# Cross-attention on one core: scores by seven block products in a reordered round

## The chip, the cores and the metric

The kernel runs on one core of a Trainium2 chip. A core has five engines, each with its own instruction list that it works through in order: PE (TensorE: matrix products, and PEld, its weight loads), DVE (VectorE), ACT (ScalarE), POOL (GpSimd) and SP (SyncE, which here issues the DMA transfers). They meet only through semaphores. The metric is the device time of one execution in microseconds (us).

## What is computed

For each of 64 batches, with x of 256 x 512, c of 256 x 384 and a hidden width H of 512, in fp32:

```python
text_p = x @ W_text + b_text
audio_p = c @ W_audio + b_audio
Q = layer_norm(text_p, g1, beta1)
K = layer_norm(audio_p, g2, beta2)
alpha = softmax(Q @ K.T / sqrt(512))
y = (alpha @ audio_p) @ W_out + b_out + x
out = layer_norm(y, g_out, beta_out)
```

## The kernel before

**Stages.** The loop `for b in range(B - 2)` is a software pipeline: round b works on five batches at once. It projects batch b+2 to its keys (`k2`) and queries (`q2`), scores batch b (`at`), forms the context of batch b-1 (`last`) and the output of batch b-2 (`old`), and normalises the output rows of batch b-3 (`settled`). Rounds 3 to 60 are alike; 0 to 2 fill the pipeline, round 61 and the code behind the loop drain it.

**Products.** The key projection and the output projection (class `Thirds`; the output's instance is `old.o`) use a scheme with 15 block products 171 columns wide instead of 18. Their parts are called `one` (into N0, N1), `two` (M0, M1), `three` (T), `four` (T, M, L) and `five` (N, M, U); N, M, L and the bank of T and U are four banks of PSUM that key and output projection share, one after the other. Steps between them (`after_one`, `after_three`, `after_four`, `after_five`) copy or combine those banks on VectorE and ScalarE; `seed` fills M with the bias. The query projection (class `Fork`) uses seven products of two chunks, 256 columns wide, in two banks: `one`, `seven`, `six`, `five`, `rest`. The sums of blocks that these schemes need on the activation side are formed on GpSimd: `Sides` (csum for the keys, zsum for the output, seven steps, L340) and `SumX` (xsum, four steps, L311). The scores (`score`, L712) are plain: 2 row tiles x 4 chunks, 256 columns wide. The context is `context_one` and `context_two` (L778). Each fp32 product appears as two instructions in the trace.

**Transposes.** The rows of q, k and e go to DRAM (`store`) and come back in squares (`fetch`, four transfers); VectorE then turns them with 32 x 32 block transposes (`turn`, `turn_e`). `affine` applies gain and shift to the turned q and k on ScalarE, chunk by chunk.

**Norms.** `rstd_of` (L400 to L404) forms the inverse root on GpSimd: a small sum, then a power of -0.5. The rows of q and k are scaled by it on ScalarE (`normalise`). An output row gets `totals` (GpSimd), `deviations` (ScalarE), `shift` (VectorE, L962), `scale_row` (ScalarE, L976) and `lift_rows` (GpSimd, L980).

**Softmax.** `maxima` (VectorE, L722), `exponentials` (ScalarE with accumulated sums, L729), `reciprocals` (VectorE, L739), `divide_e` (ScalarE, L743).

**Order.** Every engine's list is in the order of the statements, written by hand; nothing reorders it. Pools of PSUM and SBUF tiles have one to four buffers each, and the next use of a buffer waits for the readers of the last one.

Of the kernel before, what the change touches and what calls it, by code (L numbers as in the profile page):

```python
# [9 lines left out]
F32 = mybir.dt.float32  # L10
# [12 lines left out]
def kernel(  # L23
# [78 lines left out]

    ident = const.tile([P, P], F32, tag="ident", name="ident")
    make_identity(nc, ident)
    nhalf = const.tile([P, 2], F32, tag="nhalf", name="nhalf")
# [158 lines left out]
    def means(rows, n, name):  # L264

        m = const.tile([P, n], F32, tag=name, name=name)
        for k in range(n):
            junk = work.tile([P, H], F32, tag="junk", name="junk")
# [137 lines left out]

    class Projection:
# [25 lines left out]
        def square(self):  # L433

            self.var = small.tile([P, self.nt], F32, tag=f"var{self.name}", name="var")
            for t in range(self.nt):
                junk = work.tile([P, H], F32, tag="junk", name="junk")
# [8 lines left out]
        def scales(self):  # L446
            if self.centred:
                self.r = rstd_of(self.var, self.nt)
                return
# [12 lines left out]
        def normalise(self):  # L462
            for t in range(self.nt):
# [39 lines left out]
        def affine(self, gam, bet, chunks=range(HC)):  # L503
            for k in chunks:
# [6 lines left out]
                )  # L511

# [3 lines left out]
    class Thirds(Projection):  # L516
# [47 lines left out]

        def after_one(self):
            n1 = self.room("n1")
            nc.vector.tensor_copy(n1, self.N1)
            dve(self.T, self.N0, n1, ALU.subtract)

        def after_three(self):  # L570
            t = self.room("t")
            nc.vector.tensor_copy(t, self.T)
            dve(self.L0, self.M0, t, ALU.add)
            dve(self.L1, self.M1, t, ALU.subtract)

        def after_four(self):
            m = self.room("m")
            dve(m, self.M1, self.delta, ALU.subtract)
            dve(self.U, self.M0, m, ALU.subtract)

        def after_five(self):
            u, n = self.room("u"), self.room("n", 2)
            nc.scalar.copy(u, self.U)
            nc.scalar.copy(n, self.N)
            dve(middle(self.rows[:, 0]), self.T, u, ALU.add)
            dve(ends(self.rows[:, 1]), self.M, n, ALU.add)
            self.noted = u, n
# [3 lines left out]

        def last_middle(self):
            u, n = self.noted
            d = self.room("d")
            nc.gpsimd.tensor_tensor(d, n[:, 0], n[:, 1], ALU.subtract)
            nc.gpsimd.tensor_tensor(middle(self.rows[:, 1]), u, d, ALU.add)

        def leave_plus(self, x, between):
            rows = self.rows
            u, n, v = self.room("u"), self.room("n", 2), self.room("d")  # L600
            dve(n, self.M, ends(x[:, 1]), ALU.add)
            dve(u, self.U, middle(x[:, 1]), ALU.add)
            dve(v, self.N0, u, ALU.add)
            between()
            self.totals = small.tile([P, 2, 2], F32, tag="totals", name="totals")
            self.last_sum(1, 0, inner, v[:, :W1], self.N1[:, :W1], ALU.subtract)
            self.last_sum(1, 1, ends, self.N, n, ALU.add)
            u = self.room("u")
            dve(u, self.U, middle(x[:, 0]), ALU.add)
            self.last_sum(0, 0, inner, self.T[:, :W1], u[:, :W1], ALU.add)  # L610
            self.last_sum(0, 1, ends, self.L, ends(x[:, 0]), ALU.add)
# [12 lines left out]
    class Fork(Projection):  # L624
# [38 lines left out]

        def after_six(self):
            dve(self.q3, self.R, self.s7, ALU.add)
            dve(self.R, self.R, bt_step, ALU.add)
# [7 lines left out]
        def rest(self):  # L674
            self.product(3, self.R)
            self.product(2, self.q1)
            self.product(4, self.q3)

        def square(self):
            self.var = small.tile([P, 2], F32, tag="varq", name="var")  # L680
            for t in range(2):
                junk = work.tile([P, H], F32, tag="junk", name="junk")
# [8 lines left out]
        def normalise(self):  # L691
            for t in range(2):
                nc.scalar.mul(self.rows[:, t, :], fork[t], self.r[t])

    class Attention:
# [23 lines left out]

        def maxima(self):  # L720
# [3 lines left out]
        def exponentials(self):  # L724

            self.e = once.tile([P, LT, S], F32, tag="e", name=f"e_{self.b}")
            self.den = small.tile([P, LT], F32, tag="den", name="den")
            for t in range(LT):
# [12 lines left out]
        def divide_e(self):  # L741
            for t in range(LT):
# [26 lines left out]
        def context_one(self):  # L769
# [3 lines left out]
            for j in range(2):  # L773
                for s in range(ST):
                    self.context_product(self.ps_z1[:, j, :], j, s)

        def context_product(self, ps, j, s):
# [4 lines left out]
                start=(s == 0),  # L782
                stop=(s == ST - 1),
            )

        def context_two(self, s):
# [3 lines left out]
            self.context_product(self.ps_z2, 2, s)  # L790
# [14 lines left out]
        def start_products(self, tag="zsum", pool=once):  # L805

            sides = Sides(self.zT, tag, pool).add()
# [18 lines left out]
        def sums(self, lo=0, n=LT):  # L826
# [4 lines left out]
            for t in self.summed:  # L831
                junk = work.tile([P, D], F32, tag="junk", name="junk")
                nc.scalar.activation(
                    junk, self.y[:, t, :], AF.Identity, scale=-1.0 / D, accum_out=self.nm[:, t : t + 1]
                )

# [647 lines left out]
```

## Time and profile before

| | |
|---|---|
| median of 3 runs | 1369.07 us (1368.69 to 1369.11) |
| the profiled execution | 1368.85 us |
| its span, first to last instruction | 1367.1 us |
| DMA moved | 322.02 MB |
| DMA queue of SP, share of 16 engines | 79.9% |

In a row of the order of time stand the start and the length in us, the engine, the line, the operation, out<-in, shape, and how many instructions were merged; in square brackets the idle time before it and who ended it. A group row has the number of instructions, busy us, the mean of one in ns, and the idle time before them. A row of a window has the window, its length, then busy us and count of PE, PEld, DVE, ACT and POOL, the granted TensorE clock, the DMA share and GB/s. A DMA row has the size in KB and the us to landing. Matrix products are pipelined, so one instruction's length is longer than the distance from its start to the next one's; the distance is what counts.

### The profile page before, as it was taken

The page shows a single profiled execution, that of the slowest core. Times are in us where ns is not written, and L with a number is a line of the kernel's source. Part 1 is how long each engine was busy: PE and PEld are TensorE (multiplying, and loading weights), DVE is VectorE, ACT ScalarE, POOL GpSimd, SP SyncE. Part 2 cuts the span into 40 slices and gives each one's busy share as a digit, 9 for nine tenths or more (in the row PEclk, how much of TensorE's full clock was granted, in tenths as well). Part 3 has the DMA queues.
Part 4 walks back from the last instruction along what each step waited for, and adds up shares of the span by engine and source line. Part 5 has one row for each costly group of instructions (what it writes and reads, how often), then busy time and mean ns, then how long its engine had stood idle before and what let it go on. Part 6 is the DMA issues. An engine that isn't in the chain of part 4 may idle for free. (4 is left out here: it accounts for less than half of the span.)

```text
span 1367.1 us, 26408 instructions
## 1 busy us (share of the span) xinstructions
PE 1355.5 (99%) x7429; PEld 1241.0 (91%) x7429; DVE 1113.6 (81%) x2689; ACT 1089.9 (80%) x2688; POOL 1158.6 (85%) x1927
## 2 busy tenths in 40 slices
PE   9999999999999999999999999999999999999997
PEld 5889999999999999999999999999999999999995
DVE  6778888888888888888888888888888888888868
ACT  5778888888788788888888887887888888888884
POOL 5788888888888888888888888888888888888865
PEclk9999999999999999999999999999999999999999
DMA  8788878877888878788789778888887888887773
GB/s 229 215 238 252 246 233 242 242 244 233 246 242 236 244 240 249 227 250 242 240 241 248 236 236 247 234 239 245 243 245 235 242 248 237 240 238 233 220 221 107
DMA packets 449096, 322.02 MB, mean 236 GB/s; under 512 B 153781, under 2 KB 381621, under 8 KB 448950
## 3 DMA queue, kind: packets, MB, share of 16 engines
q1 hardware_dynamic: 448854, 320.20, 79.9%
q8 instruction: 60, 0.98, 0.3%
q14 instruction: 86, 0.70, 0.2%
q10 hardware_dynamic: 96, 0.13, 0.0%
HBM read 203.57 MB, written 116.65 MB: 234 GB/s over the span
## 5 line engine op out<-in xcount | busy, mean ns | idle before, releaser
L712 PE MATMUL ps_sc<-kT,qT 128*128 128x256 f32 x1024 | 260.9, 379 | 0.0
L340 POOL TENSOR_TENSOR zsum<-zsum,zT 128x256 f32<-128x256 f32 x305 | 193.4, 651 | 14.4
L712 PEld LDWEIGHTS ps_sc<-kT,qT 128*128 128x128 f32 x1024 | 186.3, 190 | 17.3 <-ACT zT L793 0.2
L778 PE MATMUL ps_z<-eT,c 128*128 128x256 f32 x768 | 186.3, 379 | 1.1 <-DVE eT L76 1.1
L644 PE MATMUL ps_f<-wtsum,xsum 128*128 128x256 f32 x756 | 183.9, 379 | 0.0
L340 POOL TENSOR_TENSOR csum<-csum,cT 128x256 f32<-128x256 f32 x310 | 172.9, 566 | 9.9
L778 PEld LDWEIGHTS ps_z<-eT,c 128*128 128x128 f32 x768 | 143.0, 190 | 18.0 <-DVE eT L76 1.5
L980 POOL TENSOR_TENSOR yr<-yr,beo 128x512 f32<-128x512 f32 x122 | 153.6, 1281 | 3.1 <-ACT yr L976 3.1
L644 PEld LDWEIGHTS ps_f<-wtsum,xsum 128*128 128x128 f32 x756 | 138.1, 190 | 14.1 <-issue 0.5
L404 POOL TENSOR_TENSOR rstd<-ve,nhalf 128x2 f32<-128x2 f32 x192 | 136.3, 710 | 16.0
L340 POOL TENSOR_TENSOR zsum<-zT 128x256 f32<-128x256 f32 x122 | 72.2, 592 | 85.3 <-ACT zT L796 85.3
L505 ACT ACTIVATE qT<-qT,columns 128x256 f32<-128x256 f32 x256 | 139.2, 594 | 2.5 <-DVE qT L76 2.5
L505 ACT ACTIVATE kT<-kT,columns 128x256 f32<-128x256 f32 x256 | 139.3, 595 | 2.0 <-DVE kT L76 1.1
L644 PE MATMUL ps_f<-wt,xT 128*128 128x256 f32 x504 | 129.4, 379 | 0.0
L729 ACT ACTIVATE e<-ps_sc,nmx 128x256 f32<-128x256 f32 x128 | 59.5, 469 | 62.8 <-DVE nmx L722 62.8
L962 DVE SCALAR_TENSOR_TENSOR yr<-yr,nm,go 128x512 f32<-128x512 f32 x124 | 104.1, 840 | 2.0 <-ACT junk L843 2.0
L644 PEld LDWEIGHTS ps_f<-wt,xT 128*128 128x128 f32 x504 | 92.9, 190 | 10.7 <-ACT ps_f L636 0.6
L514 DVE TENSOR_TENSOR ps_l<-ps_m,t 128x171 f32<-128x171 f32 x248 | 85.5, 345 | 16.9
L796 ACT COPY zT<-ps_z 128x256 f32<-128x256 f32 x64 | 23.8, 372 | 86.2 <-PE ps_z L778 86.2
L514 DVE TENSOR_TENSOR ps_f<-ps_f,s 128x256 f32<-128x256 f32 x126 | 54.5, 432 | 44.3 <-PE ps_f L644 40.9
L976 ACT ACTIVATE yr<-yr,rstd 128x512 f32<-128x512 f32 x122 | 87.4, 717 | 2.6 <-POOL rstd L404 1.1
L311 POOL TENSOR_TENSOR xsum<-xT 128x256 f32<-128x256 f32 x124 | 88.2, 733 | 0.0
(247 smaller groups left out, 3775.7 us busy)
## 6 DMA issues: line engine op xcount, KB each, us to landing
kd<-kr SPq DMA_DIRECT2D x64, 512.0 KB, 3.1
kq<-kd SPq DMA_DIRECT2D x256, 128.0 KB, 3.2
qd<-qr SPq DMA_DIRECT2D x64, 512.0 KB, 3.0
qq<-qd SPq DMA_DIRECT2D x256, 128.0 KB, 2.7
xq<-in_x_dram SPq DMA_DIRECT2D x252, 128.0 KB, 3.3
x<-in_x_dram SPq DMA_DIRECT2D x63, 512.0 KB, 4.7
out_dram<-yr SPq DMA_DIRECT2D x62, 512.0 KB, 4.0
cq<-in_ctx_dram SPq DMA_DIRECT2D x252, 96.0 KB, 3.3
```

The costliest lines, as they stand in the source:

```text
L311: self.engine.tensor_tensor(*step)
L340: nc.gpsimd.tensor_tensor(*step)
L404: nc.gpsimd.tensor_tensor(r, ve, nhalf[:, :n], ALU.pow)
L505: nc.scalar.activation(self.T[:, k, :], self.T[:, k, :], AF.Identity, bias=bet[:, k : k + 1], scale=gam[:, k : k + 1],)
L514: nc.vector.tensor_tensor(o, i0, i1, op)
L644: nc.tensor.matmul(place, lhsT=side, rhs=w, start=False, stop=True, skip_group_check=True)
L712: nc.tensor.matmul(self.sc[:, t, :], lhsT=self.q.T[:, k, bass.ts(t, P)], rhs=self.k.T[:, k, :], start=(k == 0), stop=(k == HC - 1),)
L729: nc.scalar.activation(self.e[:, t, :], self.sc[:, t, :], AF.Exp, bias=self.nmx[:, t : t + 1], accum_out=self.den[:, t : t + 1],)
L778: nc.tensor.matmul(ps, lhsT=c_rows[self.b][:, s, bass.ts(j, P)], rhs=self.eT[:, s, :], start=(s == 0), stop=(s == ST - 1),)
L962: nc.vector.scalar_tensor_tensor(row, row, self.nm[:, t : t + 1], go_sb, ALU.add, ALU.mult)
L976: nc.scalar.mul(self.y[:, t, :], self.y[:, t, :], self.r[t])
L980: nc.gpsimd.tensor_tensor(self.y[:, t, :], self.y[:, t, :], beo_sb, ALU.add)
```

## The change

Rounds 3 to 60 (`fast`) get a body of their own, in which the parts of all stages are interleaved statement by statement. In it:

- the scores are seven block products of two chunks, 128 columns wide (`score_part`). Their sums of blocks are formed on GpSimd, four of the queries in round b (`query_step`) and three of the keys one round earlier (`key_step`); PSUM blocks are copied by ScalarE (`copy_p1`, `copy_p7`) and added by VectorE (`add_p7`);
- inverse roots come from ScalarE, as exp(-0.5 ln(var + eps)) (`rstd_beside`), one pair for q and k together and one for the output; this holds in the other rounds too;
- an output row is scaled and lifted by one VectorE instruction (`settle`, the form of `shift`) in place of `scale_row` and `lift_rows`;
- the copies of N1 and T, two for the keys and two for the output, move from VectorE to ScalarE;
- the affine of the keys moves into the round before; e's fetch moves to the head of the next round.

In the diff, `y` is `old.o`. Besides, junk comes from a pool with one buffer, and the context products set their start flag once per bank. The loads, stores and fetches are as many as before. The core of the diff:

```diff
+    nc.scalar.preload_act_table_set("natural_log_exp_and_others")
...
+    def rstd_beside(var, n, by=1.0):
+        log = small.tile([P, n], F32, tag=f"log{n}", name="log")
+        nc.scalar.activation(log, var, AF.Ln, bias=eps, scale=by)
+        r = small.tile([P, n], F32, tag=f"rstd{n}", name="rstd")
+        nc.scalar.activation(r, log, AF.Exp, scale=-0.5)
+        return [r[:, t : t + 1] for t in range(n)]
...
+    def scales_of(a, b, var):
+        r = rstd_beside(var, 4)
+        a.r, b.r = r[:2], r[2:]
...
+        def copy_n1(self):
+            self.n1 = self.room("n1")
+            nc.scalar.copy(self.n1, self.N1)
+        def start_t(self):
+            dve(self.T, self.N0, self.n1, ALU.subtract)
...
-            t = self.room("t")
-            nc.vector.tensor_copy(t, self.T)
+            self.t = self.room("t")
+            nc.scalar.copy(self.t, self.T)
...
+        def key_sums(self):
+            T = self.k.T
+            t = once.tile([P, 3, 2, P], F32, tag="ksum", name="ksum")
+            b11, b12, b21, b22 = [self.block("k", j, m) for j in range(2) for m in range(2)]
+            self.ksteps = [
+                (t[:, 0:2], T[:, :, P:].rearrange("p (j c) s -> p j c s", j=2),
+                 T[:, :2, :].rearrange("p c (m s) -> p m c s", m=2), ALU.subtract),
+                (t[:, 2], b22, t[:, 0], ALU.subtract),
+                (b12, b21, t[:, 2], ALU.subtract),
+            ]
...
+        def query_sums(self):
+            s = once.tile([P, 3, 2, P], F32, tag="qsum", name="qsum")
+            a11, a21, a12, a22 = [self.block("q", j, m) for j in range(2) for m in range(2)]
+            self.steps = [
+                (s[:, 1], a11, a21, ALU.subtract),
+                (s[:, 0], a21, a22, ALU.add),
+                (s[:, 2], s[:, 0], a11, ALU.subtract),
+                (a21, a12, s[:, 2], ALU.subtract),
+            ]
...
+        def open_scores(self):
+            self.sc = p_at.tile([P, LT, S], F32, tag="at", name="ps_sc")
+            nc.vector.memset(self.sc[:, :, P:], 0.0)
+        def score_part(self, *parts):
+            for n in parts:
+                t, m = {7: (1, 1), 2: (0, 0), 4: (1, 0)}.get(n, (0, 1))
+                for c in range(2):
+                    nc.tensor.matmul(self.place(t, m), lhsT=self.qsides[n][:, c],
+                        rhs=self.ksides[n][:, c], start=False, stop=True, skip_group_check=True)
+        def copy_p1(self):
+            nc.scalar.copy(self.place(0, 0), self.place(0, 1))
+        def copy_p7(self):
+            self.s7 = once.tile([P, P], F32, tag="sc7", name="sc7")
+            nc.scalar.copy(self.s7, self.place(1, 1))
+        def add_p7(self, m):
+            dve(self.place(1, m), self.place(0, 1), self.s7, ALU.add)
...
+        if fast:
+            last.fetch_e()
+            k2.one()
+            old.context_two(0); old.context_two(1)
+            if b + 4 < B: load_c(b + 4)
+            k2.copy_n1()
+            k2.start_t()
+            old.copy_two()
+            settled.totals()
+            at.affine_queries(1)
+            cT[b + 3] = turn_c(b + 3)
+            at.affine_queries(0)
+            q2.six()
+            old.start_products(n=1)
+            k2.three()
+            k2.copy_t()
+            k2.two()
+            k2.start_l0()
+            at.affine_queries(2)
+            old.zsides.add(1)
+            q2.seven()
+            k2.start_l1()
+            at.query_sums()
+            at.query_step(0)
+            old.zsides.add(1)
+            at.affine_queries(3)
+            settled.deviation(0)
+            k2.four()
+            xT[b + 3] = turn_x(b + 3)
+            k2.take_m()
+            q2.after_seven()
+            settled.deviation(1)
+            at.query_step(1)
+            old.zsides.add(1)
+            k2.start_u()
+            k2.five()
+            k2.copy_n()
+            k2.copy_u()
+            at.open_scores()
+            q2.start_q3()
+            old.zsides.add(1)
+            at.query_step(2)
+            y.one()
+            y.copy_n1()
+            q2.step_r()
+            q2.five()
+            k2.leave_ends()
...
+            settled.last_deviation()
+            k[b + 1].turn([0])
+            k2.leave()
+            k[b + 1].turn([1])
+            y.start_t()
+            at.score_part(1, 7)
+            k2.square(var[:, 2:], [0])
+            at.copy_p1()
+            q2.after_five()
+            y.two()
+            at.copy_p7()
...
+            last.turn_e()
+            y.start_l0()
+            k2.middle_d()
+            settled.shift(1)
+            at.score_part(6)
+            at.add_p7(0)
+            q2.three()
+            settled.settle(1)
...
+            q2.square(var[:, :2], [0])
+            cs[b + 3].add(1)
+            at.score_part(3)
+            att[b + 1].affine_keys(3)
+            x_new.add(1)
+            scales_of(q2, k2, var)
+            at.score_part(2)
+            k2.normalise([0])
+            k2.normalise([1])
+            q2.normalise([0])
+            k2.seed()
...
+            at.maxima()
+            q2.normalise([1])
+            Fork.seed()
+            k2.store()
+            last.context_one()
+            settled.shift(0)
+            at.exponentials([0])
+            at.exponentials([1])
+            y.last_10()
+            at.reciprocals()
+            last.copy_one()
+            y.plus_middle(x_old, 0)
+            at.divide_e([0])
+            q2.store()
+            q3 = q[b + 3] = Fork(b + 3, x_new.of, wt_blocks)
+            q3.one()
+            x_new.add(1)
+            y.last_01(x_old)
+            k2.fetch()
...
+            y.last_00()
+            cs[b + 3].add(1)
+            Fork.clear()
+            q3.after_one()
+            at.store_e()
+            if b + 4 < B: att[b + 1].key_step(2)
+            q2.fetch()
+            settled.settle(0)
+            continue
```

More of the change, by code (lines that the diff above doesn't have):

```diff
@@ L431, in evict, with square @@
                 moments(self.mv, self.rows[:, t, :], t)
[L433 to L437, printed above, removed]
+        def square(self, var=None, tiles=range(2)):
+            if var is None:
+                var = small.tile([P, self.nt], F32, tag=f"var{self.name}", name="var")
+            self.var = var
+            for t in tiles:
+                junk = once.tile([P, H], F32, tag="junk", name="junk")
                 nc.scalar.activation(
@@ L672, in after_five, with three, two, four @@
             dve(self.q2, self.R, self.s7, ALU.add)
-        def rest(self):
[L675 to L682, printed above, removed]
+        def three(self):
+            self.product(3, self.R)
+        def two(self):
+            self.product(2, self.q1)
+        def four(self):
+            self.product(4, self.q3)
+        def rest(self):
+            self.three()
+            self.two()
+            self.four()
+        def square(self, var=None, tiles=range(2)):
+            if var is None:
+                var = small.tile([P, 2], F32, tag="varq", name="var")
+            self.var = var
+            for t in tiles:
+                junk = once.tile([P, H], F32, tag="junk", name="junk")
                 nc.scalar.activation(
@@ L722, in maxima, with exponentials @@
             nc.vector.tensor_reduce(self.nmx, self.sc, AX.X, ALU.max, negate=True)
[L724 to L728, printed above, removed]
+        def exponentials(self, tiles=range(LT)):
+            if 0 in tiles:
+                self.e = once.tile([P, LT, S], F32, tag="e", name=f"e_{self.b}")
+                self.den = small.tile([P, LT], F32, tag="den", name="den")
+            for t in tiles:
                 nc.scalar.activation(
```

334 lines of the change are left out of this document (255 added, 79 removed).

## The prediction

> **What bounds the kernel now.** I read the page first, then TensorE in order of time over one steady round, then all engines over ten rounds, then the start, where products 128 columns wide can be seen.
>
> ```profile
> span 1367.1 us, 26408 instructions
> ...
> PE 1355.5 (99%) x7429; PEld 1241.0 (91%) x7429; DVE 1113.6 (81%) x2689; ACT 1089.9 (80%) x2688; POOL 1158.6 (85%) x1927
> ```
>
> TensorE is busy for 99% of the span. A modelled duration can hide a wait, so I check the pace in the order of time:
>
> ```profile
> 303.92 0.74 PE L530 MATMUL ps_n<-wa,csum 128*128 128x171 f32 x4
> 304.50 0.74 PE L530 MATMUL ps_m<-wa,csum 128*128 128x171 f32 x4
> ...
> 306.23 1.89 PE L644 MATMUL ps_f<-wtsum,xsum 128*128 128x256 f32 x8
> 307.95 0.45 PE L530 MATMUL ps_u<-wa_thirds,csum 128*128 128x171 f32 x2
> ...
> 322.98 1.89 PE L778 MATMUL ps_z<-eT,c 128*128 128x256 f32 x8
> 324.70 0.74 PE L530 MATMUL ps_n<-wa,csum 128*128 128x171 f32 x4
> ```
>
> From start to start, four instructions of 171 columns take 0.58 us (0.145 each) and eight of 256 columns 1.72 us (0.215 each). A steady round has 56 wide ones (28 for q, 16 for scores, 12 for context) and 60 of 171 columns: 56 x 0.2155 + 60 x 0.1452 = 20.78 us, and the round lasts 324.70 - 303.92 = 20.78. TensorE issues without a gap. Whatever shortens its list pays in full, and a wait put into the list costs in full.
>
> ```profile
> 506.00:712.00 206.00, 206.00 (x1153) 191.72 (x1152) 170.78 (x417) 168.12 (x416) 179.38 (x298) 1.00 0.81 241
> ```
>
> 206 us are 9.91 rounds. So per round VectorE (third time) works 17.2 us, ScalarE 17.0 and GpSimd 18.1; each has over 2 us to spare. The granted clock is 1.00.
>
> **TensorE's part of the change.** Rounds b = 3 to 60, 58 of them, replace 16 instructions of 256 columns (8 products, two instructions each in the trace) by 7 blocks x 2 chunks x 2 = 28 of 128 columns. At full clock the trace has no such product of two ordinary operands. Nearest are the transposes of 128 columns at the start, and what follows them:
>
> ```profile
> 11.07 0.60 PE L199 MATMUL ps_rows<-ident,xTr 128*128 128x128 f32 x4
> 11.51 1.02 PE L420 MATMUL ps_l<-wa,cT 128*128 128x512 f32 x2
> ...
> 11.40 0.30 PEld L420 LDWEIGHTS ps_l<-wa,cT 128*128 128x128 f32 x2
> ...
> L644 PEld LDWEIGHTS ps_f<-wtsum,xsum 128*128 128x128 f32 x756 | 138.1, 190 | 14.1 <-issue 0.5 <-ACT wao L250 0.2 <-DVE wa_thirds L361 0.2
> ```
>
> Four transposes, each with a weight load of its own, occupy 11.07 to 11.51: 0.11 each. The ordinary load of 11.40 lets its product start at 11.51, 0.11 later; two such loads fit in 0.30 us and one lasts 0.19, so the second began 0.11 after the first. The line through 0.1452 (171 columns) and 0.2155 (256) gives 0.1096 at 128. Bounds: 0.109 below, and 0.145 above, the pace at which loads are seen to keep up for long. I take 0.1096, since both load and stream have been seen at it: 28 x 0.1096 = 3.07 against 16 x 0.2155 = 3.45. The bound of a round falls by 0.38 to 20.40 us, and 58 x 0.38 = 22.0 us go.
>
> The Trainium skill speaks against this (TensorE: Matmul & The Clock Gate, section Back-to-back issue gap): it gives 81 ns for a pair of weight load and product at 128 columns where the stream alone needs about 56, a factor of 1.45. By that factor the 28 would take 4.45 us and a round would grow by 1.0 us; the row above shows the pair at the stream's own pace, though only for a few in a row.
>
> **The other engines, per steady round.** Means of these rows:
>
> ```profile
> L962 DVE SCALAR_TENSOR_TENSOR yr<-yr,nm,go 128x512 f32<-128x512 f32 x60 | 50.4, 839 | 0.0
> L567 DVE COPY n<-ps_n 128x171 f32<-128x171 f32 x60 | 20.1, 336 | 4.2 <-PE ps_n L530 0.6
> ...
> L976 ACT ACTIVATE yr<-yr,rstd 128x512 f32<-128x512 f32 x60 | 43.0, 716 | 0.3
> L584 ACT COPY n<-ps_n 128x342 f32<-128x342 f32 x30 | 13.5, 450 | 0.0
> L583 ACT COPY u<-ps_u 128x171 f32<-128x171 f32 x30 | 9.0, 301 | 23.2 <-PE ps_u L530 23.2
> ...
> L980 POOL TENSOR_TENSOR yr<-yr,beo 128x512 f32<-128x512 f32 x60 | 75.2, 1275 | 0.0
> L404 POOL TENSOR_TENSOR rstd<-ve,nhalf 128x2 f32<-128x2 f32 x88 | 62.5, 710 | 7.3
> L311 POOL TENSOR_TENSOR xsum<-xT 128x256 f32<-128x256 f32 x59 | 41.9, 730 | 0.0
> ```
>
> GpSimd loses two lifts (2 x 1.275) and three powers (3 x 0.71), 4.68 us; the small sums ahead of the powers go too and are left out. It gains four query sums (4 x 0.73) and three key sums (1.275 for 512 elements, 2 x 0.73), 5.66. That makes at most 19.1 of 20.4 us. VectorE hands four copies to ScalarE (4 x 0.336) and gains two settles (2 x 0.84, L962's form), a memset and two 128-column sums (three at no more than 0.336): +1.3, 18.5 us. ScalarE loses two scalings (1.43), gains the four copies (1.20), two of 128 columns (at most 0.60), and four logarithms and exponentials of 2 to 4 elements, each between 0.20 (the accumulator read below) and 0.47 (an exponential of 256 elements). I take 1.0 for the four, near the small end because of their size: +1.4, 18.4 us. So no sum binds. What can cost is a late hand-over, because the new order puts producers close ahead of TensorE. I laid the new lists of the engines beside a gapless TensorE and found four places with under half a microsecond in hand.
>
> Two edits cost nothing. The scratch tile junk has one buffer instead of two, but only ScalarE writes it, in its own order, so nobody waits for it. The context products set their start flag once for two halves of a bank, with the same instructions.
>
> **First place: softmax to k2.three.** The maxima wait for score part 2. Behind them VectorE's list has shift(0), last_10, the reciprocal (which waits for both exponentials), u, last_01, last_00, the memset, settle(0) and k2's start_t, which k2.three needs. TensorE's cover is context_one, q3.one, k2.one, context_two and q2.six: 20 x 0.2155 + 4 x 0.1452 = 4.89 us.
>
> ```profile
> 321.10 0.65 DVE L722 TENSOR_REDUCE nmx<-ps_sc 128x2 f32<-128x512 f32 x1
> ...
> 323.14 0.15 DVE L739 RECIPROCAL rden<-den 128x2 f32<-128x2 f32 x1
> 323.25 0.33 DVE L614 SCALAR_TENSOR_TENSOR yr<-d,ps_n 128x170 f32<-128x170 f32 x1
> ...
> 323.63 0.52 DVE L614 SCALAR_TENSOR_TENSOR yr<-ps_n,n 128x342 f32<-128x342 f32 x1
> ...
> 324.07 0.33 DVE L514 TENSOR_TENSOR u<-ps_u,x 128x171 f32<-128x171 f32 x1
> ...
> 321.79 0.47 ACT L729 ACTIVATE e<-ps_sc,nmx 128x256 f32<-128x256 f32 x1 [1.02 <-DVE nmx L722]
> ...
> 322.25 0.47 ACT L729 ACTIVATE e<-ps_sc,nmx 128x256 f32<-128x256 f32 x1
> 322.61 0.20 ACT L729 ACTIVATION_READ_ACCUMULATOR e<-ps_sc,nmx 128x1 f32 x1
> ...
> 324.90 0.59 ACT L793 COPY zT<-ps_z 128x512 f32<-128x512 f32 x1 [0.17 <-PE ps_z L778]
> ```
>
> The context ended by TensorE's pace at 324.70 and its reader began at 324.90: 0.20 to hand over. Independent neighbours on VectorE overlap by 0.08 (0.52 long, next after 0.44). The chain: 0.20, maxima 0.69 (to the exponential's start), shift 0.76, last_10 0.38, reciprocal 0.11 (the exponentials end 0.12 before it: 322.81 - 321.10 = 1.71 against 1.83), u 0.25, last_01 0.44, last_00 0.38, memset 0.25, settle 0.76, start_t 0.34, and 0.16 for a hand-over and a weight load: 4.72. In hand: 0.17. With no overlap at all (nine times 0.08) it would be 5.44, and TensorE would stand 0.55 a round.
>
> **Second: k2.five to y.one.** y.one overwrites N, so ScalarE must have copied it: 0.20 + 0.45 + 0.16 = 0.81 against TensorE's cover of six instructions, 0.87. In hand: 0.06, if ScalarE is free. Ahead of it there stand the copy of t, two affines, two deviations and s7:
>
> ```profile
> 307.65 1.09 ACT L505 ACTIVATE kT<-kT,columns 128x256 f32<-128x256 f32 x2
> 308.65 0.71 ACT L843 ACTIVATE junk<-yr,nm 128x512 f32<-128x512 f32 x1
> ...
> 309.35 0.71 ACT L843 ACTIVATE junk<-yr,nm 128x512 f32<-128x512 f32 x1
> ```
>
> Start to start that is 1.00 for two affines and 0.70 for a deviation; with 0.3 for each copy, 3.0 us from k2.three's end, where TensorE has two, seven, four and the N pairs, 3.47, before it. ScalarE is there first.
>
> **Third and fourth.** take_m and start_u of k2 stand between k2.four's M1 and the M products of k2.five: 0.20 + 0.34 + 0.37 + 0.16 = 1.07 against eight instructions, 1.16. The copy after context_two, four zsum steps and two query steps on GpSimd must be done for y.one: 0.57 + 5 x 0.73 + 0.5 with 0.1 between each, about 5.2, against 5.5.
>
> **Queues.** DMA count is the same. On SP, k2's and q2's fetches, e's store and, now first in the next round, e's fetch follow each other.
>
> ```profile
> kq<-kd SPq DMA_DIRECT2D x256, 128.0 KB, 3.2
> ...
> 324.06 1.87 SPq L73 DMA_DIRECT2D kq<-kd  x4
> ```
>
> k2 is normalised 4.2 us before the round's end; one landing of the store (I use 3.2), two fetches (2 x 1.87), the store of e (3.2), and its fetch (1.87 + 3.2) put e's squares at 11 us into the next round, where VectorE turns them and context_one reads them at 17.8: over 5 us of cover. Without it, e's turn would hold y's L0 behind it on VectorE.
>
> **The rivals.** *Lock.* A VectorE instruction with both inputs in SBUF and a GpSimd instruction that overlaps it lengthen one another:
>
> ```profile
> 309.65 0.78 DVE L962 SCALAR_TENSOR_TENSOR yr<-yr,nm,go 128x512 f32<-128x512 f32 x1
> ...
> 309.84 0.91 POOL L340 TENSOR_TENSOR zsum<-zsum,zT 128x128 f32<-128x128 f32 x1
> ...
> 309.02 0.45 POOL L340 TENSOR_TENSOR zsum<-zsum,zT 128x128 f32<-128x128 f32 x1
> ...
> 1331.03 1.57 DVE L962 SCALAR_TENSOR_TENSOR yr<-yr,nm,go 128x512 f32<-128x512 f32 x1
> ```
>
> The same 128x128 step takes 0.45 beside nothing and 0.91 beside a shift, and a shift takes 0.78 to 1.57. The settles double the number of such instructions, and shift(0) and settle(0) stand in the softmax chain. If they lengthen that chain by 0.73 (one at 1.57 in place of 0.84), TensorE stands 0.73 - 0.17 = 0.56 a round, 0.18 more than it saves: 1368.85 + 58 x 0.18 = 1379 us, slower. It decides from 0.17 + 0.38 = 0.55 on. For it: the new settle(0) lies on the chain. Against: what GpSimd has there are 128-column steps of 0.45 and the tiny means. The Trainium skill states it as a rule (SBUF — State Buffer, section Who interferes with whom): the instruction that starts second waits for the other's end; 0.45 + 0.45 in the row above agrees.
>
> *Thin waits.* The same places cost 0.2 to 0.3 a round (a copy or chain that comes 0.25 later than in my sums): 1346.9 + 58 x 0.25 = 1361, still faster.
>
> *Weight loads bind.* At 0.145 for each of the 28, a round grows by 4.06 - 3.45 = 0.61: 1404. For it: no long run at 0.11 in the trace; against: the load that served after 0.11.
>
> *The change does not do what it says*: logarithm and exponential could swap ScalarE's table. The program built from the changed kernel has one table load, as the one before, so I give it 1%.
>
> **How the numbers follow.** The profiled execution took 1368.85 us (span 1367.1, 1.8 around it), 0.2 below the median of the runs. Less 22.0 that is 1346.9. Rounds 0 to 2 and 61 keep eight products; round 2 makes the next round's keys besides its own, up to 2 us once or nothing. For the four thin places I add 0.05 a round, 2.9 us, because slacks of 0.06 to 0.17 are as small as the errors of my sums: 1350. Chances: this forecast, 1345 to 1356, 0.64; thin waits 0.2; lock 0.11; weight loads 0.04; tables 0.01. The range 1344 to 1364 takes the first and most of the second. About 0.2% can be told from no change; between thin waits and lock 0.04 falls within it, so faster 0.83, same 0.04, slower 0.13.
>
> **What would show it.** Score instructions at 0.11 start to start; a round of 20.4 to 20.5; no wait of TensorE before k2.three or y.one. I am wrong if the 28 go at more than 0.123 each (3.45/28), or if ps_u or ps_n shows waits of 0.4 a round on VectorE or ScalarE.

## The result, and the profile after

The change made the kernel 1.2% slower: 1384.88 us (median of 4 runs, 1383.83 to 1385.81) against 1368.88 (4 runs, 1368.49 to 1369.11). The ratio is 1.0117, 95% interval 1.0099 to 1.0135. The profiled execution took 1384.61 us.

The page of the changed kernel: span, busy time of each engine, and the first group row, the one that grew most.

```profile
span 1382.8 us, 28546 instructions
...
PE 1360.8 (98%) x8125; PEld 1245.9 (90%) x8125; DVE 1195.5 (86%) x2733; ACT 1166.7 (84%) x3188; POOL 1159.2 (84%) x1838
...
L1144 DVE SCALAR_TENSOR_TENSOR yr<-yr,nm,go 128x512 f32<-128x512 f32 x124 | 201.5, 1625 | 1.0 <-ACT junk L1025 1.0
```

TensorE's busy time went up by 5.3 us although its list needs less time at full pace: a modelled duration hides waits, so the page alone doesn't show them. L1144 is `shift`, L962 before. On the page before, its mean was 840 ns; it is now 1625.

Where the 15.7 us of span came from can be read off the start of `k2.one` in rounds 4 and 61, before and then after (order of time, TensorE):

```profile
116.83 0.74 PE L530 MATMUL ps_n<-wa,csum 128*128 128x171 f32 x4
...
1301.89 0.74 PE L530 MATMUL ps_n<-wa,csum 128*128 128x171 f32 x4
```

```profile
125.66 0.74 PE L548 MATMUL ps_n<-wa,csum 128*128 128x171 f32 x4
...
1313.40 0.74 PE L548 MATMUL ps_n<-wa,csum 128*128 128x171 f32 x4
```

Up to round 4 the kernel lost 8.8 us. The 57 rounds between lost 2.7 (1187.74 against 1185.06). Behind round 61's start it lost 4.2 (69.4 us to the end of the span against 65.2). So there are two questions: why steady rounds gained nothing, and what happened outside them.

**A steady round.** TensorE in one round of the changed kernel, in the order of time:

```profile
668.02 0.74 PE L548 MATMUL ps_n<-wa,csum 128*128 128x171 f32 x4
...
676.41 0.61 PE L867 MATMUL ps_sc<-kT,qT 128*128 128x128 f32 x4
...
682.08 0.74 PE L548 MATMUL ps_l<-wao_thirds,zT 128*128 128x171 f32 x4
682.72 0.71 PE L867 MATMUL ps_sc<-ksum,qsum 128*128 128x128 f32 x4
683.27 0.74 PE L548 MATMUL ps_n<-wao_thirds,zsum 128*128 128x171 f32 x4
683.99 0.85 PE L548 MATMUL ps_m<-wao_thirds,zT 128*128 128x171 f32 x4
684.68 0.45 PE L548 MATMUL ps_u<-wao_thirds,zT 128*128 128x171 f32 x2
684.97 1.50 PE L867 MATMUL ps_sc<-kT,qT 128*128 128x128 f32 x12
686.30 1.89 PE L945 MATMUL ps_z<-eT,c 128*128 128x256 f32 x8
...
688.90 0.74 PE L548 MATMUL ps_n<-wa,csum 128*128 128x171 f32 x4
```

The twelve score instructions from 684.97 last 1.33 us to the next product: 0.111 each. The round takes 20.88 us; the products alone, 40 x 0.2155 + 60 x 0.1452 + 28 x 0.111 is 20.44. What is missing lies at one spot. Four 171-column instructions should take 0.58 and four of the scores 0.44; from 682.08 to 684.97 the steps are 0.64, 0.55, 0.72 and 0.69, which is 0.06 + 0.11 + 0.14 + 0.11 too much. Score part 5 (682.72) and `y.five`'s products into M (683.99) start late.

What they wait for stands on VectorE (order of time, changed kernel):

```profile
679.80 2.65 DVE L1144 SCALAR_TENSOR_TENSOR yr<-yr,nm,go 128x512 f32<-128x512 f32 x1
682.38 0.29 DVE L532 TENSOR_TENSOR ps_sc<-ps_sc,sc 128x128 f32<-128x128 f32 x1
682.58 0.74 DVE L1153 SCALAR_TENSOR_TENSOR yr<-yr,rstd,beo 128x512 f32<-128x512 f32 x1
683.24 0.32 DVE L532 TENSOR_TENSOR m<-ps_m,bao_delta 128x171 f32<-128x171 f32 x1
683.59 0.34 DVE L532 TENSOR_TENSOR ps_u<-ps_m,m 128x171 f32<-128x171 f32 x1
```

and on GpSimd in the same microseconds:

```profile
679.80 0.73 POOL L343 TENSOR_TENSOR csum<-csum,cT 128x256 f32<-128x256 f32 x1
680.48 0.74 POOL L314 TENSOR_TENSOR xsum<-xsum,xT 128x256 f32<-128x256 f32 x1
681.17 0.73 POOL L343 TENSOR_TENSOR csum<-csum,cT 128x256 f32<-128x256 f32 x1
683.57 1.28 POOL L849 TENSOR_TENSOR ksum<-kT 128x512 f32<-128x512 f32 x1 [1.66 <-ACT rstd L415]
```

`shift(1)` begins at 679.80 together with the first of three sums that follow each other without a gap (none needs the one just before it), and ends at 682.45, half a microsecond after the third. Alone it would take 0.74 (the settle at 682.58 has the same form). Behind it in VectorE's list stand `add_p7(0)`, which part 5 needs, `settle(1)`, and then `y.take_m` and `y.start_u`, which free M for `y.five`. The view of the waits shows the two late hand-overs with their counts (total us, times, longest):

```profile
PEld ps_m L548 <- DVE ps_u L532: 12.9, 53, 0.3
...
PEld ps_sc L867 <- DVE ps_sc L532: 5.2, 29, 0.7
```

53 of the 58 rounds show the late M. In the other five (17, 35, 43, 51 and 59) `shift(1)` takes 1.26 us, and just these five last 20.46 us. One of them (VectorE, then GpSimd):

```profile
784.15 1.26 DVE L1144 SCALAR_TENSOR_TENSOR yr<-yr,nm,go 128x512 f32<-128x512 f32 x1
...
784.13 0.74 POOL L343 TENSOR_TENSOR csum<-csum,cT 128x256 f32<-128x256 f32 x1
784.82 1.19 POOL L314 TENSOR_TENSOR xsum<-xsum,xT 128x256 f32<-128x256 f32 x1
```

The three sums are the same and come at the same distance, but here VectorE gets in behind the first of them, and the second is the one that waits. So the changed kernel itself shows what the long `shift(1)` costs. The 57 rounds above have 52 long ones and these five: 52 x 20.87 + 5 x 20.46 = 1187.5, against 1187.74 measured.

**Outside the steady rounds.** The page of waits has `PE ps_u L548 <- DVE ps_u L532` with seven waits of TensorE. One of them, in round 61 (ScalarE, VectorE and TensorE in the order of time):

```profile
1324.66 0.74 PE L548 MATMUL ps_n<-wao,zsum 128*128 128x171 f32 x4
...
1325.43 0.63 ACT L451 ACTIVATE junk<-kr 128x512 f32<-128x512 f32 x1
...
1326.24 0.63 ACT L451 ACTIVATE junk<-kr 128x512 f32<-128x512 f32 x1
...
1327.00 0.30 ACT L413 ACTIVATE log<-var,eps 128x4 f32<-128x4 f32 x1
1327.33 0.20 ACT L415 ACTIVATE rstd<-log 128x4 f32<-128x4 f32 x1
1327.44 0.28 ACT L585 COPY n<-ps_n 128x171 f32<-128x171 f32 x1
...
1327.75 0.34 DVE L532 TENSOR_TENSOR ps_u<-ps_n,n 128x171 f32<-128x171 f32 x1 [2.88 <-ACT n L585]
...
1328.24 0.53 PE L548 MATMUL ps_u<-wao_thirds,zsum 128*128 128x171 f32 x2 [1.40 <-DVE ps_u L532]
```

`y.one` ends near 1325.4. Its N1 would be copied at once by VectorE, which idles for 2.88 us; ScalarE copies it at 1327.44, behind two squares of the keys, their accumulator reads and the root. The statement order of these rounds is nearly the old one, but `after_one` and `after_three`, which all rounds share, now copy on ScalarE. Read off the pace in the same way there are eight such delays, 5.3 us up to round 4 and 4.1 at the end, 9.4 us together.

### The profile page after: what moved, and what is told of

Its sections match the earlier page's. It is cut to its first block, busy times and chain, and to the rows that moved or that the text cites. A ratio compares the mean times of both kernels' runs of the same rounds, so it can differ in the third digit from the quotient of the medians.

```text
span 1382.8 us, 28546 instructions
## 1 busy us (share of the span) xinstructions
PE 1360.8 (98%) x8125; PEld 1245.9 (90%) x8125; DVE 1195.5 (86%) x2733; ACT 1166.7 (84%) x3188; POOL 1159.2 (84%) x1838
## 4 chain that ended last, share of the span: by engine, by line
PE 89%; DMA 3%; ACT 3%; DVE 3%; SPq 1%; issue 1%; DVEq 0%; POOL 0%; ACTq 0%
PE ps_f L721 26%; PE ps_m L548 16%; PE ps_sc L867 14%; PE ps_z L945 11%; PE ps_n L548 10%; PE ps_u L548 8%; PE ps_l L548 5%; DMA qd<-qr 1%; SPq L73 1%; DMA wo<-in_L_xattn_W_out_dram 1%; ACT junk L451 1%; DMA kd<-kr 0%; ACT junk L777 0%; DVE yr L1144 0%; DMA wt<-in_L_xattn_W_text_dram 0%
## 5 line engine op out<-in xcount | busy, mean ns | idle before, releaser
L1144 DVE SCALAR_TENSOR_TENSOR yr<-yr,nm,go 128x512 f32<-128x512 f32 x124 | 201.5, 1625 | 1.0 <-ACT junk L1025 1.0
L343 POOL TENSOR_TENSOR zsum<-zsum,zT 128x256 f32<-128x256 f32 x305 | 170.5, 568 | 5.3
L849 POOL TENSOR_TENSOR ksum<-kT 128x512 f32<-128x512 f32 x58 | 73.9, 1274 | 97.9 <-ACT rstd L415 88.1
L532 DVE TENSOR_TENSOR ps_l<-ps_m,t 128x171 f32<-128x171 f32 x248 | 83.4, 336 | 52.7 <-PE ps_m L548 44.5
L867 PE MATMUL ps_sc<-kT,qT 128*128 128x128 f32 x928 | 122.3, 275 | 0.0
L867 PEld LDWEIGHTS ps_sc<-kT,qT 128*128 128x128 f32 x928 | 119.2, 192 | 3.0
L867 PE MATMUL ps_sc<-ksum,qsum 128*128 128x128 f32 x696 | 111.2, 282 | 0.4 <-DVE ps_sc L532 0.4
L867 PEld LDWEIGHTS ps_sc<-ksum,qsum 128*128 128x128 f32 x696 | 96.1, 191 | 11.4 <-DVE ps_sc L532 5.2
L990 POOL TENSOR_SCALAR nm<-totals 128x1 f32<-128x1 f32 x124 | 70.1, 580 | 38.7 <-DVE yr L691 38.7
L343 POOL TENSOR_TENSOR csum<-cT 128x256 f32<-128x256 f32 x124 | 96.6, 779 | 6.6 <-DVE cT L76 6.6
L1153 DVE SCALAR_TENSOR_TENSOR yr<-yr,rstd,beo 128x512 f32<-128x512 f32 x120 | 85.8, 717 | 0.0
```

Source lines behind the costliest of these rows:

```text
L343: nc.gpsimd.tensor_tensor(*step)
L532: nc.vector.tensor_tensor(o, i0, i1, op)
L849: nc.gpsimd.tensor_tensor(*self.ksteps[n])
L867: nc.tensor.matmul(self.place(t, m), lhsT=self.qsides[n][:, c], rhs=self.ksides[n][:, c], start=False, stop=True, skip_group_check=True,)
L990: nc.gpsimd.tensor_scalar(self.nm[:, j : j + 1], t[:, 0, j : j + 1], t[:, 1, j : j + 1], -1.0 / D, ALU.add, ALU.mult)
L1144: nc.vector.scalar_tensor_tensor(row, row, self.nm[:, t : t + 1], go_sb, ALU.add, ALU.mult)
```

## The experiments

Ratios are against the kernel before, run beside each on the same chip (its medians there were 1368.44 to 1369.13 us); "round" is the distance of `k2.one` from one steady round to the next.

| run | what | us | ratio (95%) | round |
|---|---|---|---|---|
| changed kernel | | 1384.88 | 1.0117 (1.0099 to 1.0135) | 20.87 |
| e2_one_sbuf_input | `shift(1)` with one SBUF input | 1362.95 | 0.9956 (0.9941 to 0.9971) | 20.46 |
| e3_shifts_moved | `shift(1)`, `settle(1)` later | 1365.07 | 0.9970 (0.9959 to 0.9981) | 20.46 |
| e9_sum_order | two GpSimd sums swapped | 1363.60 | 0.9963 (0.9948 to 0.9978) | 20.46 |
| e1_copies_back | copies back on VectorE outside | 1378.19 | 1.0062 (1.0047 to 1.0077) | 20.87 |
| e4_both | e1 and e3 | 1357.78 | 0.9914 (0.9898 to 0.9931) | 20.46 |
| e5_old_roots_outside | e4, outside roots on GpSimd | 1354.96 | 0.9902 (0.9886 to 0.9919) | 20.46 |
| e6_plain_scores_new_order | e4 with eight plain products | 1375.73 | 1.0051 (1.0036 to 1.0066) | 20.79 |
| e7_settle_apart | e4 without the one-step settle | 1473.42 | 1.0768 (1.0752 to 1.0784) | 22.55 |
| e8_steady_roots_gpsimd | e4 with steady roots on GpSimd | 1437.33 | 1.0503 (1.0487 to 1.0518) | 21.87 |
| e10_best | e5 and two small moves | 1353.69 | 0.9889 (0.9873 to 0.9906) | 20.46 |

### The stall in the steady round: three ways to take it away

**One SBUF input.** If `shift(1)` is long because GpSimd's sums keep it from its inputs, an instruction with one input in PSUM, at the same place and of the same size, should not wait.

```diff
-            settled.shift(1)
+            settled.shift_beside(1)
...
+        def shift_beside(self, t):
+            gain = Thirds.M0[:, :P].rearrange("p (o h) -> p o h", o=1).broadcast_to([P, 4, P])
+            row = self.y[:, t, :].rearrange("p (o h) -> p o h", o=4)
+            nc.vector.scalar_tensor_tensor(
+                row, row, self.nm[:, t : t + 1], gain, ALU.add, ALU.mult
+            )
```

> Edit: in the steady rounds the first output shift, shift(1), reads its gain from a PSUM block in place of the SBUF row of gains, so it has one SBUF input; same place, same size, wrong gain for that tile (the output of that half is not the reference's). Theory (lock: two SBUF inputs make it stand 1.9 us behind three GpSimd sums in a row): the instruction takes about 0.75 us in place of 2.65, score part 5 and y.five no longer wait, the round falls from 20.87 to about 20.46: 1384.9 - 58 x 0.38 = 1363. It stays possible that settle(1) is caught in its place, then 1363 to 1370. Rival (the place in the list or a late GpSimd result makes it long, not the second input): 2.65 us and 1385 stay.

Group row of `shift(1)` in this kernel (the 620 us from 300 on), and from the order of time a settle behind it:

```profile
L1155 DVE SCALAR_TENSOR_TENSOR yr<-yr,nm,ps_m 128x512 f32<-128x512 f32 x31 | 22.5, 727 | 0.0
```

```profile
670.94 1.68 DVE L1160 SCALAR_TENSOR_TENSOR yr<-yr,rstd,beo 128x512 f32<-128x512 f32 x1
```

0.73 in place of 2.65 us, and 21.9 us off the kernel. The block passed to `settle(1)`, which has two SBUF inputs and takes 1.68; but it starts early enough to hold nobody up, and the round is at 20.46.

**The same instructions later.** If the length itself does no harm, only what is queued behind it, moving it should do as well.

```diff
             k2.start_t()
+            if done: done.settle(1)
...
-            settled.shift(1)
             at.score_part(6)
             at.add_p7(0)
+            settled.shift(1)
             q2.three()
-            settled.settle(1)
...
+            if b + 4 == B: settled.settle(1)
```

`settle(1)` now runs one round later, behind `k2.start_t`; the last of these rounds makes its own at its end.

> Edit: nothing of the work changes; in the steady rounds shift(1) stands behind add_p7(0) instead of ahead of it, and settle(1) moves into the next round behind k2's start_t, where VectorE sat idle for 0.8 us. Theory (lock): shift(1) may still stand up to 1.1 us behind GpSimd, but nobody on TensorE waits for it; round 20.46 to 20.5, 1362 to 1364 us. Rival (VectorE has too much work in the round): the wait moves to another TensorE user, the round stays at 20.8 or more, 1380 or more.

VectorE in this kernel:

```profile
669.15 0.30 DVE L532 TENSOR_TENSOR ps_sc<-ps_sc,sc 128x128 f32<-128x128 f32 x1 [0.65 <-PE ps_sc L867]
669.36 1.89 DVE L1144 SCALAR_TENSOR_TENSOR yr<-yr,nm,go 128x512 f32<-128x512 f32 x1
671.18 0.32 DVE L532 TENSOR_TENSOR m<-ps_m,bao_delta 128x171 f32<-128x171 f32 x1
```

`shift(1)` still takes 1.89 us, but `add_p7(0)` is ahead of it, `settle(1)` is gone, and nobody waits: 19.8 us less than the changed kernel. It is the place in the list that costs.

**Only GpSimd's order.** VectorE's and TensorE's lists stay as the change has them; one `x_new.add(1)` moves from ahead of `scales_of` to behind the csum sum that follows `k2.seed()`, so that the two csum sums become neighbours, of which the second needs the first.

```diff
-            x_new.add(1)
             scales_of(q2, k2, var)
...
             k2.seed()
             cs[b + 3].add(1)
+            x_new.add(1)
```

> Edit, on the changed kernel itself: of the three GpSimd sums that stand beside shift(1), the second (an xsum step) and the third (a csum step) change places; nothing else. The csum step needs the result of the csum step before it, so a gap of about 0.08 us opens between them; before, the next sum began before the last had ended. Theory (GpSimd keeps the lock as long as its next sum is already in line, and VectorE gets it in the first gap): shift(1) takes 0.7 + 0.75 = about 1.4 us in place of 2.65, the round falls to 20.46, 1384.9 - 57 x 0.39 = 1363. Rival (VectorE waits for the whole run of sums, up to the wait ahead of the key sums): 2.65 us and 1385 stay.

GpSimd and then VectorE in this kernel at the same place of a round:

```profile
730.20 1.86 POOL L343 TENSOR_TENSOR csum<-csum,cT 128x256 f32<-128x256 f32 x2
732.02 1.18 POOL L314 TENSOR_TENSOR xsum<-xsum,xT 128x256 f32<-128x256 f32 x1
...
730.21 1.27 DVE L1144 SCALAR_TENSOR_TENSOR yr<-yr,nm,go 128x512 f32<-128x512 f32 x1
```

Now `shift(1)` gets in after the first sum (1.27), and it is GpSimd that waits: two sums take 1.86 instead of 1.41 (0.73 behind a start 0.68 later). 1363.60 us: the swap of two sums on an engine with time to spare is worth 21.3 us. That the dependent sum leaves a moment (0.08 us) in which VectorE gets its turn is my reading; the runs show the order and its effect. It can't be the whole rule: in this kernel `settle(1)` (731.60, 1.01 us) goes ahead of the xsum sum at 732.02, which needs nothing of the sum before it and follows without a gap, and in the changed kernel VectorE got in behind the first sum in five rounds with no such moment. What decides the turn stays open.

### Outside the steady rounds

**Copies back.** In `after_one` and `after_three`, which the steady rounds do not call:

```diff
-            self.copy_n1()
+            self.n1 = self.room("n1")
+            nc.vector.tensor_copy(self.n1, self.N1)
...
-            self.copy_t()
+            self.t = self.room("t")
+            nc.vector.tensor_copy(self.t, self.T)
```

> Edit: in the rounds that keep the old order (0 to 2, 61, and behind the loop) the copies of N1 and T go back to VectorE; the 58 steady rounds stay as in the changed kernel. Theory (these copies were moved to ScalarE everywhere because a shared helper was edited, and there they stand behind long work): the waits of ps_u and ps_m outside the steady rounds, 0.95 + 0.94 + 0.34 + 1.48 + 1.57 + 1.57 + 1.70 + 0.80 = 9.4 us, go: about 1375.5 us. Rival (the logarithm pair on ScalarE or the settles on VectorE make those rounds late): within 2 us of 1384.9.

6.7 of the 9.4 us came back, and steady rounds stayed at 20.87, as they should. The periods of rounds 0 and 1 shrank only from 18.39 and 18.32 to 18.08 and 17.98 (16.46 and 17.01 before), so something else is late there. Together with e3's moves:

> Edits of e1 and e3 together. Theory: both gains add, 1384.9 - 22 - 9.4 = 1353 us, below the kernel before by 16 us. Rivals as in e1 and e3: 1362 or more if the first edit brings nothing, 1375 or more if the second brings nothing.

27.1 us below the changed kernel where the two alone sum to 26.5: the two gains add. 4.8 are missing to what I expected; by the traces they lie in about equal parts in the steady rounds (20.3 in place of 22), up to round 4 (3.6 in place of 5.3) and at the end (2.4 in place of 4.1).

**Roots.** VectorE at the start of e4_both, with the three weight sums and the first step of a bias:

```profile
38.78 2.32 DVE L365 TENSOR_TENSOR wa_thirds<-wa_thirds,wa 128x171 f32<-128x171 f32 x3
41.03 1.23 DVE L224 SCALAR_TENSOR_TENSOR part<-wo,columns,bo 128x512 f32<-128x512 f32 x1
```

The kernel before has 1.45 us for the same three and 0.75 for the step. With roots on ScalarE, GpSimd is free of its powers and runs its xsum sums at 38.51 instead of 43.18, beside VectorE's sums, and each holds the other up. The experiment puts the roots of rounds 0 to 2 and behind the loop back on GpSimd (`rstd_of`), separate for q and k.

```diff
-                self.r = rstd_beside(self.var, self.nt)
+                self.r = rstd_of(self.var, self.nt)
...
+        q2.scales()
...
-        scales_of(q2, k2, var)
+        k2.scales()
...
```

> Edit, on top of the kernel of e4 (1357.8): outside the 58 steady rounds the roots are formed on GpSimd again, q's and k's apart, at their old places. Theory: with the roots on ScalarE, GpSimd no longer waits for them and runs its query sums 4.7 us earlier, beside VectorE's two-input instructions of the start, which lengthen (three weight sums 2.32 us in place of 1.45, the first bias part 1.23 in place of 0.75), and the common root of q and k makes Fork's seed 0.75 us late in round 0; both go: 1354 to 1356. Rival (what is left outside the steady rounds, 6 us, comes from the new work of round 2 and the change of order at round 3 alone): within 1 us of 1357.8.

VectorE in this kernel:

```profile
38.90 1.49 DVE L365 TENSOR_TENSOR wa_thirds<-wa_thirds,wa 128x171 f32<-128x171 f32 x3
40.31 0.97 DVE L224 SCALAR_TENSOR_TENSOR part<-wo,columns,bo 128x512 f32<-128x512 f32 x1
```

The sums are back to 1.49 and the step is at 0.97; the periods of rounds 0 and 1 go from 17.90 and 17.75 to 17.46 and 17.02, and round 4 starts 1.9 us earlier. The medians differ by 2.8 us, but they are from two chips and their intervals overlap, so I go by the 1.9.

### What each part of the change is worth

**Eight plain products in the new order**: e4 without the seven products, with `score` at the places of `score_part`.

> Edit, on top of e4: in the steady rounds the scores are the eight plain products again, at the places of the seven parts; query sums, key sums, the two copies and the two sums of blocks are left out. All else of the new order stays. Theory: TensorE sets the round and its list grows from 28 x 0.1115 = 3.12 to 16 x 0.2155 = 3.45: a round of 20.79, 1357.8 + 58 x 0.33 = 1377. Rival (the new order itself, not the products, shortened the round): below 1370.

The round is 20.79, that of the kernel before. So the order shortens nothing by itself, and the seven products are worth 0.33 us a round (the medians, 1375.73 and 1357.78, from two chips, differ by 18 us, which is 0.31 for each of 58 rounds).

**Settle apart**: e4 with `scale_row` and `lift_rows` in place of each `settle`.

> Edit, on top of e4: in the steady rounds each settle is a scaling on ScalarE and a lift on GpSimd again. Two VectorE instructions with two SBUF inputs go, GpSimd gets 2 x 1.275 us more: 17.7 + 2.55 = 20.2 us of a round of 20.46. Theory (GpSimd then has no time left for its waits and becomes late for TensorE): round 20.9 or more, 1383 or more. Rival (the lock is the main burden, and without the settles things run easier): 1357 to 1360.

**Steady roots on GpSimd**: e4 with `rstd_of` in `scales_of` and `last_deviation`.

> Edit, on top of e4: in the rounds the roots are formed on GpSimd again (a small sum and a power of -0.5, one pair for q and k, one for the output). GpSimd gets about 2 x (0.71 + 0.4) = 2.2 us more, 19.9 of 20.46. Theory (the logarithm and exponential were needed to make room on GpSimd): late sums and a round of 20.6 to 21, 1366 to 1389. Rival (GpSimd sits idle for 1.7 us before the key sums and takes the root of q and k there at no cost): within 3 us of 1357.8.

The waits of the weight loads and a row of GpSimd's order of time in e7, and then the waits and the window of ten rounds in e8:

```profile
PEld ps_n L548 <- POOL zsum L343: 81.5, 58, 1.7
PEld ps_m L548 <- DVE ps_l L532: 20.1, 58, 0.4
```

```profile
685.73 2.53 POOL L1164 TENSOR_TENSOR yr<-yr,beo 128x512 f32<-128x512 f32 x2 [1.44 <-ACT yr L1160]
```

```profile
PEld ps_f L723 <- ACT ps_f L715: 40.1, 59, 1.7
PEld ps_m L548 <- DVE ps_l L532: 14.8, 57, 0.3
PEld ps_n L548 <- POOL zsum L343: 14.4, 58, 1.9
PEld ps_n L548 <- POOL csum L343: 14.4, 57, 0.3
```

```profile
506.00:712.00 206.00, 203.36 (x1210) 181.87 (x1208) 162.93 (x403) 162.87 (x433) 200.06 (x310) 1.00 0.79 229
```

Both cost more than I expected. In e7 GpSimd idles 1.44 us for ScalarE's scaling and then lifts for 2.53 before the first zsum sum can run at 688.67, and `y.one` waits for a zsum sum in 58 rounds, 1.4 us each. In e8 GpSimd is busy for 200.06 of 206 us and four hand-overs are late; how the one that ScalarE ends goes back to GpSimd was not followed. At this order, neither the one-step settle nor the roots on ScalarE can be left out; that they pay by making room on GpSimd for the block sums fits these rows. Other places for the old steps weren't tried.

### A version that beats both

e5, with two of the key sums for round 3 moved behind that round's query sums, and the last `settle(1)` behind round 61's `k2.after_three`:

```diff
+            if b == 3: at.key_step(1); at.key_step(2)
...
         k2.after_three()
+        if not three:
+            done.settle(1)
...
-                for n in range(3):
-                    att[b + 1].key_step(n)
+                att[b + 1].key_step(0)
```

> Edit, on top of e5 (1355.0): of the three key sums for round 3 two move from the end of round 2 to behind round 3's query sums, and the last settle(1) moves behind round 61's after_three. Theory: the two waits that the trace of e5 shows there, 1.75 us for zsum in round 3 and 0.95 us for ps_u in round 61, go: 1352 to 1353.5. Rival (the sums are late there for another reason): 1354.5 to 1355.5.

1353.69 us, 1.1% below the kernel before. Against e5 that is 1.3 us with overlapping intervals; in the traces the span is shorter by 1.5 (1353.1 and 1351.6). Its busy time over ten rounds:

```profile
506.00:712.00 206.00, 206.00 (x1288) 195.49 (x1288) 182.02 (x434) 182.48 (x505) 186.87 (x293) 1.00 0.85 245
```

## Why the prediction was wrong

I forecast 1350 us and a gain; the sum went wrong by 35 us: some 21 at the lock, 13 outside the steady rounds and 2.9 at the score term, less the 2.9 that I had put down for thin places and that nothing used. Of the signs that I had named, the length of the round alone (20.87) showed it; the waits were at M and at score part 5, where I had not looked.

**The score term: right in kind, a little too large.** 28 instructions at 0.1096 should have saved 0.38 a round. They run at 0.111 and the round reaches 20.46, a saving of 0.33: 58 x 0.05 = 2.9 us less. The rival that weight loads bind is out: twelve in a row held 0.111. The factor of 1.45, worked out from the figures of the Trainium skill (TensorE: Matmul & The Clock Gate, section Back-to-back issue gap), does not hold for these products.

**The lock: the right mechanism, at the wrong place and the wrong size.** This step failed most. I looked for the block where I had found little slack, in the softmax chain, and took "one at 1.57 in place of 0.84", a wait for one GpSimd instruction. There nothing happened: no wait before `k2.three`; `settle(0)` takes 0.67, and `shift(0)` about 0.86. I never worked out what stands behind `shift(1)`, because I had asked which new instruction was on a thin path, not which blocked one had a thin path behind it. It was an old instruction, moved ahead of `add_p7(0)`, `y.take_m` and `y.start_u`, while GpSimd got a run of three sums there; and in 53 of 58 rounds it waits for all three, mostly 2.65 us instead of 0.74. 0.41 a round in some 52 rounds are 21 us; e2, e3 and e9 each give 20 to 22 back by a different edit, and the five rounds in which it did not wait so long last 20.46, so this is shown. That 1379 lies near the measured time is chance: it was made of 0.18 a round in the softmax chain and nothing outside.

The Trainium skill says that, of a VectorE instruction with two SBUF inputs and a GpSimd one that reads SBUF, the one that starts first keeps the shared port pair for its whole instruction and the other fully blocks (SBUF — State Buffer, section SBUF: two separate sides). The trace agrees that it blocks, but a wait for one sum would make 0.73 + 0.74 = 1.47 at most, and about 2.65 was measured in 53 rounds: the next sum went ahead of the waiting VectorE, twice. My "0.45 + 0.45" was no such check: that sum stands 0.59, to the shift's end at 310.43, and is done 0.32 later, as `shift(1)` is done 0.55 behind the third sum and not 0.74.

**The four thin hand-overs held.** I checked softmax to `k2.three`, `k2.five` to `y.one`, take_m and start_u of k2, and zsum to `y.one`. In the stalled round TensorE goes from 668.02 to 676.41 in 8.39 us, just what 34 x 0.1452 + 16 x 0.2155 makes. But my third place has a twin, the same two steps of the output, and that one failed; I had not listed it. e7 shows the fourth failing once GpSimd has the lifts ahead of it.

**Engine sums held.** For GpSimd, VectorE and ScalarE I had at most 19.1, 18.5 and 18.4 us a round. The window of e10_best is 10.07 rounds and gives 18.6, 18.1 and 18.1; in the changed kernel itself VectorE has 18.8, with the waiting of `shift(1)` counted as work. Logarithm and exponential take 0.30 and 0.20, so 1.0 for two pairs, as taken. No engine binds.

**"Rounds 0 to 2 and 61 ... up to 2 us once or nothing": this step failed.** It was 13 us (8.8 and 4.2). I had looked at the products of these rounds only. The edit to `after_one` and `after_three` is in helpers that they share, and ScalarE's order there was written when it had no such copy to make: 9.4 us, of which e1 gave 6.7 back. The roots outside the steady rounds cost another 2 (e5). The late sums that I had allowed for are there too: in round 3 `y.one` waits 1.4 us for a zsum sum. In e10 the time up to round 4 is still 1.3 us above that of the kernel before (118.16 against 116.83), and the end 0.7; I did not follow these further.

**Queues, transfers and tables held**: in 30 steady rounds one wait of 0.2 us is put down to a DMA, and the logarithm stands 0.33 us ahead of the exponential, with no room between them for a table load, of which the trace has one, 1.28 us long, at the start.

With both faults mended the change does nearly what TensorE's list says: 57 rounds at 0.33 are 18.8 us, and in e10 they give 17.5 (1167.57 us against 1185.06).

## What to carry to other kernels

When VectorE instructions with two SBUF inputs are moved or added, lay them beside GpSimd's list at that time: count the whole run of sums ahead of its next gap as a wait that can happen, and ask who is queued behind the blocked one. When an edit sits in a helper, walk every caller, the rounds that keep the old order above all; a copy is only as early as the list of the engine that makes it. A modelled busy share of 98% says nothing about waits of 2%: compare the distance between starts with the products' own pace.

## What the runs showed of the hardware

The contention of VectorE and GpSimd is not shared out in turns. The form of `shift` takes 0.74 us beside nothing. Beside three GpSimd sums of 0.73 that follow without a gap, `shift(1)` waited for all three in 53 of 58 rounds, 2.65 in most of them, and took 1.26 in five; it took 1.27 where the second sum needs the first, and 0.73 beside the same sums if one of its inputs is in PSUM. These runs don't show what decides whose turn it is. An order of two sums on an engine with 12% idle time moved the kernel by 21.3 us. And an fp32 product of two instructions 128 columns wide keeps 0.111 us for each, twelve in a row, its weight loads hidden.
